# Three expert slots instead of six fetched beside the scatter of rows, and empty slots written during the second FFN

## The chip, the core and the metric

The kernel runs on one NeuronCore of a Trainium2 chip. The core has a matrix engine, TensorE (PE in the profile; its weight loads are listed apart as PEld), and VectorE (DVE), ScalarE (ACT), GpSimd (POOL) and SyncE (SP). Each engine takes its instructions in order from its own queue[...]. Transfers between memory and the on-chip buffers are done by 16 DMA engines[...]. SP does no arithmetic here and issues most of the transfers; ACT issues a few.

The metric is the device time of one execution in microseconds (us); for a kernel, the median of its runs.

## The reference

Four layers act on x, of 2 sequences, 1024 tokens each and 256 features (2048 tokens in all), in fp32. Every layer does

```
xn = layernorm(x)
x  = x + attention(xn) + ffn(xn)
```

with another attention and another FFN each time:

- layer 0: rotary attention with 16 heads of 16 features, and a gated FFN with 1024 hidden features (silu(gate) * up, then down)
- layer 1: rotary attention with 16 query heads and 4 key heads of 128 features, and again a gated FFN with 1024 hidden features
- layer 2: a state-space layer, and an FFN with weights rounded to -1, 0 and 1
- layer 3: an attention with states and actions of 32 features, and a mixture of 16 experts

The mixture of experts, cut to what matters:

```python
logits = x @ router_w
top_vals, top_ids = jax.lax.top_k(logits, 2)
probs = jax.nn.softmax(top_vals, axis=-1)
...
for e in range(16):
    h = silu(x @ W1[e]) @ W2[e]          # 256 -> 512 -> 256
    out = out + combine[:, e:e + 1] * h  # combine: probs at top_ids, else 0
```

Each token thus needs only two of the 16 experts.

## The kernel before, in words

x stays in the on-chip buffer in 16 tiles of 128 tokens (`xs`), worked on in four blocks of 512 tokens. A framework turns the Python loops into one queue for each engine, inserts the semaphores, and may reorder instructions by its own estimates, except between layers (`tc.no_sync_barrier()`) and where an order is asked for (`keep_in_program_order`, used for PE in layers 1 and 3).

**Norms.** `norm` (lines 95 to 122) takes for each block the statistics of four tiles on DVE (L102, L103), a square root on ACT (L105), a reciprocal on DVE (L107), the normalised tiles xn on DVE (L111), eight transposes on PE (L119) and two copies on ACT (L120) into `xnT`, the operand of the matmuls that follow.

**Gated FFN.** `ffn` (lines 160 to 181) runs over the four blocks; in each over eight "heads" of 128 hidden features: two matmuls into `g` (PSUM, tag "A", two buffers), two into `u` (tag "S", two buffers), the silu of g on ACT (L172) and the product with u on DVE (L174). Then the down projection and the addition to x (L132) follow. Layer 1's FFN is called by `swiglu(1, xnT, gu1, dn1)` at line 794, behind the whole attention of layer 1, whose last steps on ACT are the copies `oT` (L701). Ahead of that call SP is given the loads of layer 2's weights (lines 770 to 792).

**Experts.** Layer 3 spends matmuls only on the pairs of a token and one of its two experts, 4096 of them. The pairs are sorted into 47 slots of 128 rows; one slot belongs to one expert. `sent` is a tensor in memory with 47 * 128 rows of 258 numbers: 256 features, the row's number and its place. The parts:

- *Empty rows.* Not every row of a slot gets a pair. So `sent` is filled with empty rows long before: `none`, a tile of zeros, is written to all 47 slots (6016 KB), and `nowhere`, the two numbers of an empty row, behind it (47 KB). In the kernel before, this stands ahead of the norm of layer 1 (lines 558 to 565): three small POOL instructions and two transfers issued by ACT. The second transfer waits until the first has landed.
- *Scatter.* `send` (L1471) has POOL issue 32 indirect transfers, each of 128 rows to their places in `sent`. Around it, PE works on the attention of layer 3 for the second sequence (`attend(1, ...)`, softmax parts at L147 to L157, x at L1557).
- *Weights and rows.* `fetch(s)` has SP read the number of slot s's expert from the on-chip buffer (`value_load`) and load that expert's two weights, 512 KB each (`we<-in_L_W` at L56), into one of the seven buffers of the pool "ring". `rows_of(s)` has SP load the slot's 128 rows from `sent` (`xg<-sent`, 129 KB, five buffers); it waits for all 32 sends.
- *The loop.* Step s loads rows three slots ahead and weights six slots ahead, transposes the rows of slot s on PE (`tokens`), does the first matmul of slot s - 1 (`up`, hp, silu on ACT) and the second of slot s - 2 (`back`, eo, and an indirect transfer of the result rows into `done`). PE, held in program order (L1309, L1312), does this behind the attention of the second sequence's first four tiles. At the end the rest of the attention follows, and `collect` (L1721) adds the two results of every token to x.

Before the loop, all of SP's early transfers are asked for in this order:

```python
for s in range(6):
    fetch(s)
for s in range(3):
    rows_of(s)
```

Of the kernel before, what the change touches and what calls it, by code (L numbers as in the profile page):

```python
# [21 lines left out]
F32, I32, U32 = mybir.dt.float32, mybir.dt.int32, mybir.dt.uint32  # L22
# [5 lines left out]
P = 128  # L28
B, T, D = 2, 1024, 256
# [4 lines left out]
NSLOT = 47  # L34
# [5 lines left out]
C_ROW, C_NONE = 776, 778  # L40
# [5 lines left out]
def kernel(ctx: ExitStack, tc: tile.TileContext, a: dict, out: bass.AP):  # L46
    nc = tc.nc
    V, S, G, PE = nc.vector, nc.scalar, nc.gpsimd, nc.tensor
# [22 lines left out]
    cst = kept("cst", [P, C_COLS])  # L71
# [17 lines left out]
    sent = dram.tile([NSLOT * P, ROW], F32, tag="sent", name="sent")  # L89
# [48 lines left out]
    def work_pool(name):  # L138
        return tc.tile_pool(name=name, bufs=2, reuse_waits="tile")
# [57 lines left out]
    def swiglu(layer, xnT, gu, dn):  # L197
        with work_pool(f"ffn{layer}") as pool, psum_pool(f"ffn{layer}_ps") as psum:
            ffn(
                pool, psum, xnT, layer, [P] * 8,  # L200
                lambda k, h: gu[k][:, h * P : (h + 1) * P],
                lambda k, h: gu[k][:, 1024 + h * P : 1024 + (h + 1) * P],
                lambda h: dn[:, h, :],
                AF.Silu,
            )
# [12 lines left out]
    with work_pool("l0n") as pool, psum_pool("l0n_ps") as psum:  # L218
        _, xnT = norm(pool, psum, 0, 5)
    with work_pool("l0") as pool, tc.tile_pool(  # L220
        name="l0_ps", bufs=1, space=PSUM, reuse_waits="tile"
# [57 lines left out]
        def fetch(b, g):  # L279
            both = []  # L280
            for w_ in range(2):
                t_ = pool.tile([P, T], F32, tag="qk", name=f"qk{b}_{g}_{w_}", bufs=8)
                G.memset(t_, float(w_))
                for j in range(4):
                    load(t_[32 * j + 1 : 32 * j + 17, :], turned[b][w_].rearrange("(r h) t -> h r t", h=16)[4 * g + j])
                both.append(t_)
            qk[b, g] = both
# [267 lines left out]


    with work_pool("l1n") as pool, psum_pool("l1n_ps") as psum:
        none = pool.tile([P, D], F32, tag="none", name="none", bufs=1)
        G.memset(none, 0.0)
        nowhere = pool.tile([P, NSLOT, 2], F32, tag="nowhere", name="nowhere", bufs=1)  # L560
        G.memset(nowhere, -P)
        G.tensor_copy(nowhere[:, :, 0], cst[:, C_NONE : C_NONE + NSLOT])
        slots = sent.rearrange("(s p) d -> p s d", p=P)
        nc.scalar.dma_start(out=slots[:, :, :D], in_=none.unsqueeze(1).to_broadcast([P, NSLOT, D]))
        nc.scalar.dma_start(out=slots[:, :, D:], in_=nowhere)
        V.tensor_scalar_mul(w1k, w1k, 1.0 / math.sqrt(128.0))
        _, xnT = norm(pool, psum, 1, 5)
    with work_pool("l1") as pool, tc.tile_pool(
        name="l1_ps", bufs=1, space=PSUM, reuse_waits="tile"
# [3 lines left out]
        gu1, dn1 = load_swiglu(a["L1_gu"], a["L1_dn"], 1)  # L573
# [217 lines left out]
    load(nwD, a["L2_nwD"])  # L791
    nw, Dp = nwD[:, 0:16], nwD[:, 16:32]

    swiglu(1, xnT, gu1, dn1)
    tc.no_sync_barrier()


# [4 lines left out]
    with work_pool("l2n") as pool, psum_pool("l2n_ps") as psum:  # L802
        _, xnT = norm(pool, psum, 2, 5)
    with work_pool("l2") as pool, tc.tile_pool(
        name="l2_ps", bufs=2, space=PSUM, reuse_waits="tile"
# [509 lines left out]
    with work_pool("l3") as pool, tc.tile_pool(  # L1315
        name="l3_ps", bufs=2, space=PSUM, reuse_waits="tile"
# [315 lines left out]
        with work_pool("l3w") as wp:  # L1632
            with tc.tile_pool(name="at0_ps", bufs=2, space=PSUM, reuse_waits="tile") as psum:
                for _ in attend(0, psum, wp, range(QT)):
                    pass
                p1, p2 = shares()
                for _ in attend(1, psum, wp, range(4)):
                    pass

            with tc.tile_pool(name="moe_ps", bufs=2, space=PSUM, reuse_waits="tile") as psum:  # L1640
                w1s, w2s, xgTs, ehs = {}, {}, {}, {}

                def fetch(s):
                    ex = nc.sync.value_load(whoi[0:1, s : s + 1], min_val=0, max_val=15)
                    we = slot(f"we{s}")
                    w1s[s], w2s[s] = part(we, 0, 2, 512), part(we, 1024, 4, D)
                    load(w1s[s], a["L3_W1"][bass.ds(ex, 1)].rearrange("e (k p) m -> p (e k) m", p=P))
                    load(w2s[s], a["L3_W2"][bass.ds(ex, 1)].rearrange("e (k p) m -> p (e k) m", p=P))

                xgs, rows3 = {}, {}  # L1650

                def rows_of(s):
                    xgs[s] = wp.tile([P, ROW], F32, tag="xg", name=f"xg{s}", bufs=5)
                    load(xgs[s], sent[s * P : (s + 1) * P, :])

                def tokens(s):
                    xg = xgs.pop(s)
                    tp = psum.tile([P, 2, P], F32, tag="X", name=f"xgp{s}")
                    for k in range(2):
                        pe_t(tp[:, k, :], xg[:, k * P : (k + 1) * P])  # L1660
                    xgTs[s] = wp.tile([P, 2, P], F32, tag="xgT", name=f"xgT{s}", bufs=3)
                    V.tensor_copy(xgTs[s], tp)  # L1662

                    row = wp.tile([P, 1], F32, tag="row", name=f"row{s}", bufs=6)
                    G.tensor_scalar(
                        row, xg[:, D + 1 : D + 2], cst[:, C_ROW : C_ROW + 1], float(s * P),
                        op0=ALU.subtract, op1=ALU.is_equal,
                    )
                    G.tensor_scalar(
                        row, row, float(B * T), xg[:, D : D + 1], op0=ALU.mult, op1=ALU.add  # L1670
                    )
                    rows3[s] = wp.tile([P, 1], U32, tag="rowi", name=f"rowi{s}", bufs=10)
                    G.tensor_copy(rows3[s], row)

                def up(s):
                    hp = psum.tile([P, 4, P], F32, tag="H", name=f"hp{s}")
                    for h in range(4):
                        for k in range(2):
                            pe(hp[:, h, :], w1s[s][:, k, h * P : (h + 1) * P], xgTs[s][:, k, :], k == 0, k == 1)
                    ehs[s] = wp.tile([P, 4, P], F32, tag="eh", name=f"eh{s}", bufs=3)  # L1680
                    S.activation(ehs[s], hp, AF.Silu)

                def back(s):
                    op = psum.tile([P, D], F32, tag="E", name=f"eo{s}")
                    for h in range(4):
                        pe(op, ehs[s][:, h, :], w2s[s][:, h, :], h == 0, h == 3)
                    y = wp.tile([P, D], F32, tag="ey", name=f"ey{s}", bufs=8)
                    V.tensor_copy(y, op)
                    it = G.indirect_dma_start(
                        out=done, out_offset=bass.IndirectOffsetOnAxis(ap=rows3.pop(s)[:, 0:1], axis=0),  # L1690
                        in_=y, in_offset=None, bounds_check=2 * B * T + NSLOT * P - 1, oob_is_err=False,
                    )

                    tc.declare_no_dep(it.ins, group="results", reason="rows of different places")
                    tc.add_to_no_dep_group("results", it.ins)

                for s in range(6):
                    fetch(s)
                for s in range(3):
                    rows_of(s)  # L1700
                for s in range(NSLOT + 2):
                    if s + 3 < NSLOT:
                        rows_of(s + 3)
                    if s + 6 < NSLOT:
                        fetch(s + 6)
                    if s < NSLOT:
                        tokens(s)
                    if 0 <= s - 1 < NSLOT:
                        up(s - 1)
                    if s - 2 >= 0:  # L1710
                        back(s - 2)

            with tc.tile_pool(name="at1_ps", bufs=2, space=PSUM, reuse_waits="tile") as psum:

                ways = done[: 2 * B * T, :].rearrange("(r i p) d -> p i r d", r=2, p=P)

                def collect(i):
                    y = wp.tile([P, 2, D], F32, tag="back", name=f"back{i}", bufs=4)
                    load(y, ways[:, i])
                    for r, pr_ in enumerate((p2, p1)):  # L1720
                        V.scalar_tensor_tensor(  # L1721
                            xs[i], y[:, r], pr_[:, i : i + 1], xs[i], op0=ALU.mult, op1=ALU.add
                        )
                    nc.scalar.dma_start(out=osrc[i], in_=xs[i])

                for _ in attend(1, psum, wp, range(4, QT)):
                    pass
                for i in range(NT):
                    collect(i)
# [115 lines left out]
```

## Time and profile before

| | us |
|---|---|
| median of 3 runs | 3138.37 |
| the three runs | 3139.37, 3131.97, 3138.37 |
| the profiled execution | 3154.62 |
| its span (first to last instruction) | 3152.9 |

The profile is of one execution, and it is that execution's own time, not the median, to which its parts add up. Its TensorE clock was granted at 0.974 of full speed on the mean. It gives for each engine the busy time, the tenths of 40 equal slices in which it was busy, groups of equal instructions by source line, the waits by what ended them, and a timeline. "ACT L105 <- DMA sent<-none" is to be read as: the instruction of line 105 on ACT waited, and what came last was the transfer from `none` to `sent`. "remote" stands for a semaphore whose sender the profile does not name. In a timeline, a bracket at the end of a row holds the idle time of the engine ahead of that instruction and what ended it. Names end in q where an engine's queue of transfers is meant (SPq, ACTq).

Where the stretches of the change lie in the span:

| stretch | from, us | to, us |
|---|---|---|
| fill of `sent` to the first projection of layer 1 | 678 | 717 |
| FFN of layer 1 | 1670 | 1835 |
| scatter of rows | 2866 | 2913 |
| loop of experts on PE, first transposes | 2943 | |

### The profile page before, as it was taken

To read this page: it belongs to the slowest core of one execution; us is meant where nothing else is said; L and a number is where in the kernel's file an instruction comes from. 1 tells how busy PE (TensorE), PEld (TensorE's weight loads), DVE (VectorE), ACT (ScalarE), POOL (GpSimd) and SP (SyncE) were. 2 spreads that over 40 slices of the span, in tenths; PEclk is the share of its full clock that TensorE was granted. 3 is DMA by queue.
4 is the path that set the end of the run, shared out by engine and by line. 5 is a ranking of instruction groups with operands and counts; after the bars stand their busy time and mean duration, and the time that the engine had idled before them with its cause. 6 is when DMAs were issued, how large, how long until landed. Compare 5 with 4: busy or idle time off the path is not lost. (4 is left out here: it accounts for less than half of the span.)

```text
span 3152.9 us, 44146 instructions
## 1 busy us (share of the span) xinstructions
PE 2929.5 (93%) x16906; PEld 1996.2 (63%) x16906; DVE 1747.9 (55%) x3889; ACT 1198.4 (38%) x2129; POOL 911.2 (29%) x1224
## 2 busy tenths in 40 slices
PE   6999999969999999999999978999999999995998
PEld 5666666545655655655655555777777778554897
DVE  5665655326566566666551167677867774333223
ACT  2023333322333333333441155766666664212111
POOL 2021010103333333333320024444444443114342
PEclk9999999978999999999999988999999999998999
DMA  5000010050000000000000010000000000004696
GB/s 156 1 28 14 1 54 1 1 133 14 1 1 1 1 1 1 1 1 14 34 1 18 1 40 1 1 1 1 1 1 1 1 19 8 10 1 145 210 352 213
DMA packets 89442, 116.93 MB, mean 37 GB/s; under 512 B 13424, under 2 KB 70704, under 8 KB 87696
## 3 DMA queue, kind: packets, MB, share of 16 engines
q1 hardware_dynamic: 68768, 93.32, 9.1%
q10 hardware_dynamic: 16672, 10.40, 1.3%
q0 software_dynamic: 3792, 10.39, 0.9%
q8 instruction: 134, 2.20, 0.3%
q14 instruction: 76, 0.62, 0.1%
HBM read 91.20 MB, written 22.89 MB: 36 GB/s over the span
## 5 line engine op out<-in xcount | busy, mean ns | idle before, releaser
L157 ACT ACTIVATE pr<-sc,nmax 128x896 f32<-128x896 f32 (+7 forms) x272 | 201.2, 740 | 477.8 <-DVE nmax L156 376.8
L671 POOL TENSOR_SCALAR pr<-pr,r,gate 128x1024 f32<-128x1024 f32 (+7 forms) x256 | 209.8, 821 | 564.0 <-DVE r L670 536.1
L576 PE MATMUL sc<-kT,qT 128*128 128x512 f32 (+3 forms) x768 | 292.3, 492 | 21.5 <-ACT pr L157 21.5
L576 PE MATMUL op<-pT,v 128*128 128x512 f32 x576 | 292.9, 595 | 1.8 <-DVE pT L688 1.2
L342 ACT ACTIVATE pT<-sc 128x1024 f32<-128x1024 f32 (+1 forms) x160 | 150.1, 938 | 270.0 <-PE sc L248 270.0
L576 PEld LDWEIGHTS sc<-kT,qT 128*128 128x128 f32 x768 | 138.5, 192 | 157.0 <-issue 123.2
L156 DVE TENSOR_REDUCE nmax<-sc 128x1 f32<-128x896 f32 (+7 forms) x272 | 205.1, 757 | 7.9
L579 PEld LDWEIGHTS tp<-cst,pr 128*128 128x128 f32 x1152 | 140.2, 141 | 99.4 <-issue 70.6
L932 DVE SCALAR_TENSOR_TENSOR xp_ps<-xp,w2r,xp_ps 128x256 f32<-128x256 f32 x320 | 153.5, 486 | 56.7 <-ACT xp_ps L831 49.3
L248 PE MATMUL sc<-qk,qk 32*128 32x256 f32 (+1 forms) x1280 | 168.2, 380 | 9.4 <-ACT pT L342 8.8
L154 DVE TENSOR_TENSOR sc<-sc,cst 128x128 f32<-128x128 f32 x272 | 79.8, 296 | 174.1 <-PE sc L576 156.8
L957 POOL TENSOR_TENSOR dm<-cst,dA 128x512 f32<-128x512 f32 x128 | 133.3, 1050 | 112.1 <-PE lp L825 84.0
L579 PE MATMUL tp<-cst,pr 128*128 128x128 f32 x1152 | 164.3, 273 | 0.7 <-POOL pr L671 0.7
L345 POOL TENSOR_SCALAR_AFFINE_SELECT pT<-pT 128x512 f32<-128x512 f32 x64 | 40.6, 634 | 427.3 <-ACT pT L342 423.9
L248 PE MATMUL mx<-qk,qk 32*128 32x256 f32 (+1 forms) x1280 | 145.3, 389 | 10.8 <-DVE qk L329 2.9
L248 PEld LDWEIGHTS sc<-qk,qk 32*128 32x128 f32 x1280 | 104.4, 185 | 66.4 <-issue 31.2
L825 PE MATMUL lp<-dm,cst 128*128 128x512 f32 x256 | 132.5, 634 | 12.2 <-DVE ml L1022 7.0
L831 ACT ACT_TABLE_LOAD x105 | 134.7, 1283 | 4.8 <-PE zp L825 2.9
L831 ACT ACTIVATE xp<-xp_ps,w2r 128x256 f32<-128x256 f32 x160 | 90.2, 564 | 121.2 <-PE xp_ps L825 98.3
L825 PE MATMUL xp_ps<-xnT,w2x 128*128 128x256 f32 x512 | 128.5, 396 | 7.2 <-DVE xx L932 3.6
L688 ACT COPY pT<-tp 128x512 f32<-128x512 f32 x160 | 93.8, 586 | 105.0 <-PE tp L579 105.0
L576 PE MATMUL m<-w1o,oT 128*128 128x256 f32 x512 | 123.7, 385 | 4.1 <-DVE t2q L604 3.4
(321 smaller groups left out, 6025.3 us busy)
## 6 DMA issues: line engine op xcount, KB each, us to landing
we<-in_L_W SPq DMA_DIRECT2D x94, 512.0 KB
xg<-sent SPq DMA_DIRECT2D x47, 129.0 KB
sent<-none ACTq DMA_DIRECT2D x1, 6016.0 KB
gu<-in_L_gu SPq DMA_DIRECT2D x4, 1024.0 KB
back<-done SPq DMA_DIRECT2D x16, 256.0 KB
x<-in_x ACTq DMA_DIRECT2D x16, 128.0 KB
dn<-in_L_dn SPq DMA_DIRECT2D x2, 1024.0 KB
tabs<-in_L_rope SPq DMA_DIRECT2D x2, 1024.0 KB
```

The lines of the kernel that those rows point to most:

```text
L156: V.tensor_reduce(nmax, sc[:, :n], axis=AX.X, op=ALU.max, negate=True)
L157: S.activation(pr, sc[:, :n], AF.Exp, bias=nmax, accum_out=total)
L248: tc.keep_in_program_order(PE.matmul(out_, lhsT=lhsT, rhs=rhs, start=first, stop=last))
L342: S.activation(pT[:, :, :, :w], sc[:, :, :, :w], AF.Exp, scale=0.25)
L576: tc.keep_in_program_order(PE.matmul(out_, lhsT=lhsT, rhs=rhs, start=first, stop=last))
L579: tc.keep_in_program_order(PE.transpose(out_, in_, ident))
L671: G.tensor_scalar(pr[:, :n], pr[:, :n], r, gate[:, i, 4 * g + j : 4 * g + j + 1], op0=ALU.mult, op1=ALU.mult,)
L688: (V.tensor_copy if kb % 2 else S.copy)(made[kb], tp)
L825: tc.keep_in_program_order(PE.matmul(out_, lhsT=lhsT, rhs=rhs, start=first, stop=last))
L831: tc.keep_in_program_order(S.activation(*args, **kw))
L932: V.scalar_tensor_tensor(dst[:, n] if k == 2 else pp[:, n], xp[:, n, k : k + 256], cw[:, c : c + 1], pp[:, n], op0=ALU.mult, op1=ALU.add,)
L957: G.tensor_tensor(dm, le.unsqueeze(1).to_broadcast([P, 4, P]), dAc[:, 4 * g : 4 * g + 4].unsqueeze(2).to_broadcast([P, 4, P]), ALU.mult,)
```

## The change

Two things are changed. The filling of `sent` with empty rows is taken out of the norm of layer 1 and put around the FFN of layer 1, in a pool of its own; the instructions are the same. And of the first six slots' weights, three are asked for ahead of the first three slots' rows and three behind them.

```diff
     with work_pool("l1n") as pool, psum_pool("l1n_ps") as psum:
-        none = pool.tile([P, D], F32, tag="none", name="none", bufs=1)
-        G.memset(none, 0.0)
-        nowhere = pool.tile([P, NSLOT, 2], F32, tag="nowhere", name="nowhere", bufs=1)
-        G.memset(nowhere, -P)
-        G.tensor_copy(nowhere[:, :, 0], cst[:, C_NONE : C_NONE + NSLOT])
-        slots = sent.rearrange("(s p) d -> p s d", p=P)
-        nc.scalar.dma_start(out=slots[:, :, :D], in_=none.unsqueeze(1).to_broadcast([P, NSLOT, D]))
-        nc.scalar.dma_start(out=slots[:, :, D:], in_=nowhere)
         V.tensor_scalar_mul(w1k, w1k, 1.0 / math.sqrt(128.0))
         _, xnT = norm(pool, psum, 1, 5)
...
-    swiglu(1, xnT, gu1, dn1)
+    with work_pool("empty") as pool:
+        none = pool.tile([P, D], F32, tag="none", name="none", bufs=1)
+        G.memset(none, 0.0)
+        nowhere = pool.tile([P, NSLOT, 2], F32, tag="nowhere", name="nowhere", bufs=1)
+        G.memset(nowhere, -P)
+        G.tensor_copy(nowhere[:, :, 0], cst[:, C_NONE : C_NONE + NSLOT])
+        slots = sent.rearrange("(s p) d -> p s d", p=P)
+        nc.scalar.dma_start(out=slots[:, :, :D], in_=none.unsqueeze(1).to_broadcast([P, NSLOT, D]))
+        nc.scalar.dma_start(out=slots[:, :, D:], in_=nowhere)
+        swiglu(1, xnT, gu1, dn1)
     tc.no_sync_barrier()
...
-                for s in range(6):
+                for s in range(3):
                     fetch(s)
                 for s in range(3):
                     rows_of(s)
+                for s in range(3, 6):
+                    fetch(s)
                 for s in range(NSLOT + 2):
```

## The prediction

> **What bounds it now.** I read the page first. In the excerpt, "xN" counts instructions, and the row DMA gives the mean busy share of the 16 DMA engines in 40 slices of 78.8 us.
>
> ```profile
> span 3152.9 us, 44146 instructions
> ...
> PE 2929.5 (93%) x16906; PEld 1996.2 (63%) x16906; DVE 1747.9 (55%) x3889; ACT 1198.4 (38%) x2129; POOL 911.2 (29%) x1224
> ...
> DMA  5000010050000000000000010000000000004696
> ...
> sent<-none ACTq DMA_DIRECT2D x1, 6016.0 KB
> ```
>
> PE is the bound: 223 us of the span are not PE's. The change touches no arithmetic, so it can only fill or open gaps of PE. The DMA engines are busy at the start, at the norm of layer 1 (the ninth slice, where `sent<-none` lies) and from the 37th slice on, where rows are scattered and expert weights fetched. So I looked at PE's gaps in three stretches: norm 1, FFN 1, scatter.
>
> **Norm 1.** The view of waits from 660 to 720 us (total, times, longest), then ACT's timeline there (start, duration):
>
> ```profile
> ACT L105 <- DMA sent<-none: 28.0, 1, 28.0
> ...
> PE ln_ps L119 <- DVE xn L111: 19.9, 3, 16.7
> ```
> ```profile
> 678.02 0.39 ACTq L564 DMA_DIRECT2D sent<-none  x1
> 703.48 0.38 ACTq L565 DMA_DIRECT2D sent<-nowhere  x1
> 703.94 1.28 ACT L105 ACT_TABLE_LOAD   x1 [27.98 <-DMA sent<-none]
> 705.24 0.49 ACT L105 ACTIVATE sd<-mv,eps 128x4 f32<-128x4 f32 x2
> ```
>
> ACT issues the 6 MB fill, then must issue `nowhere`, which waits for the fill's completion; the square roots stand behind both. PE waits 16.7 us for xn, which needs them.
>
> *Gain of moving it.* DVE has x complete at 690.1. A block's four statistics take 1.74 us (0.87 a pair), so the first root could run at 692, with its table loaded before. Then DVE is the limit: 16 statistics and aggregates 7.0 us, 16 xn 5.5 (1.38 per four), four reciprocals 0.7, the w1k scale 0.7, together 13.9: 704 without gaps, 705.5 with the small waits before now between blocks. The last xn ends at 715.5 now. **Gain 10 us (9 to 11).** Behind it, the attention's tables are loaded when the norm frees their space and move with it; they now stand ahead of gu1 in SP's queue, not behind, which matters little: gu1 is used 950 us later. The memsets before the fill move on POOL to behind the last probability scaling (L671), where nothing waits for POOL.
>
> **FFN 1.** By the order of instructions in the changed kernel, the two fills stand on ACT directly behind the last copy of attention 1 (L701) and ahead of the silu table load and all 32 silus. ACT and PE in that stretch:
>
> ```profile
> 1666.79 0.58 ACT L701 COPY oT<-op 128x512 f32<-128x512 f32 x1 [2.64 <-PE op L576]
> 1667.39 1.28 ACT L172 ACT_TABLE_LOAD   x1
> 1671.96 0.60 ACT L172 ACTIVATE sg<-g 128x512 f32<-128x512 f32 x1 [3.29 <-PE g L129]
> ```
> ```profile
> 1669.94 1.98 PE L129 MATMUL g<-xnT,gu 128*128 128x512 f32 x4 [0.52 <-DVE x L132]
> 1671.76 1.88 PE L129 MATMUL u<-xnT,gu 128*128 128x512 f32 x4
> 1673.48 1.88 PE L129 MATMUL g<-xnT,gu 128*128 128x512 f32 x4
> ...
> 1676.91 1.88 PE L129 MATMUL g<-xnT,gu 128*128 128x512 f32 x4
> ```
>
> The last row is the third head; g and u have two PSUM buffers each, so it needs the first silu's read. *Cost, in the times of before:* the fill goes out at 1667.4. From its issue to the first activation behind `nowhere` was 27.2 us in norm 1 (705.24 - 678.02), table load included; the load beside it was 1 MB then, and w2z and the small tables, 1.35 MB, now. First silu 1694.6, done 1695.2; PE's third head starts at 1695.3 instead of 1676.9: **18.4 us**, 19.4 with the larger load beside. PE then restarts at half clock: after the two gaps of the scatter below, 4.4 and 5.2 us of its work ran so, half of it lost, 2.2 to 2.6 us. Nothing is won back: PE bounds FFN 1 (3.43 us per head, against 0.60 on ACT and 0.69 on DVE). **Cost 20.6 to 22, say 21.3; the net of the move is +11.3 us** (+9.6 to +13). A faster or slower fill moves both ends alike down to the point at which norm 1's gap closes, so the net hardly depends on it.
>
> Here a rule speaks for a shorter fill. The Trainium skill, "DMA: Bandwidth & Descriptors", section "Specifications", gives the transfers a ceiling of 435 GB/s. 6.16 MB would take 14.2 us; the row says 25.1 (678.4 to 703.5), 245 GB/s. With the ceiling, 10.9 us less, cost 10.4 and norm gain none, as DVE would free it: +10. I take the row.
>
> **Scatter.** POOL sends 32 times 128 rows from 2866.4 to 2907.9, 1.28 us each; SP issues weights beside it, 12 transfers of 512 KB, the first four at 2869.8 to 2872.5. Waits from 2866 to 2945, and stretches (time, then busy us of PE, PE's loads, DVE, ACT, POOL; clock, DMA share, GB/s):
>
> ```profile
> PE op L1309 <- DVE pT L149: 16.7, 2, 15.9
> ...
> PE op L1309 <- ACT pT L147: 14.7, 4, 13.5
> DVE x L1557 <- remote: 13.8, 2, 7.9
> ...
> DVE sc L154 <- remote: 9.8, 1, 9.8
> ```
> ```profile
> 2878.00:2893.00 15.00, 0.00 (x0) 0.00 (x0) 1.02 (x3) 0.89 (x2) 11.34 (x13) 0.59 0.87 288
> 2893.00:2900.00 7.00, 6.21 (x17) 4.32 (x17) 0.31 (x2) 0.00 (x0) 5.48 (x6) 0.66 0.74 248
> 2900.00:2913.00 13.00, 0.03 (x1) 0.03 (x1) 1.98 (x6) 1.58 (x3) 6.04 (x8) 0.67 0.53 168
> ```
>
> PE stands still for 15.9 + 13.5 = 29.3 us, and with the half clock loses 34. DVE and ACT wait there for semaphores that arrive 8 to 10 us after the matmul has ended ("remote"). *What three slots less can gain:* nothing if the scatter alone holds the semaphores up. If the weights do, not all 34: the first row tile now comes at 2942.95, and rows cannot be there before the last send lands and is fetched, about 2915. So **0 to 28 us in the profiled execution.** In timed runs less: plain register moves of SP take 0.69 us there instead of 0.03, which looks like the recording of the trace being held up, and the profiled run, 3154.6 us (1.7 outside its span), is 16.3 over the median. If that excess lies here, some 12 us remain at most.
>
> A rule speaks against any gain: "SBUF — State Buffer", section "SBUF: two separate sides", holds that engine ports and DMA ports are disjoint and neither slows the other. By it, this part is worth 0. The row shows late semaphores at a high DMA share, but the share alone is not the cause: the stall goes on at 0.53 (third row), with weights nearly done, and in the loop of experts the share is 0.89 over 176 us with PE busy for 175.9. Nearest to the stall, then, is the scatter, which stays. I take 0 to 2, **1 us**.
>
> *What it costs:* slots 3 to 5 now wait in SP's queue behind the rows, which wait for all sends: issued at 2912.6 instead of by 2910. At the loop's pace (1.31 MB per 3.73 us, 351 GB/s) 3.1 MB land by 2922; slot 3 is used three slots of 3.73 us after the first, 2926 at the earliest. Cover 4 us or more; nothing.
>
> **Sum.** -10 + 21.3 - 1 = +10.3. On the profiled run's own time 3165; on the median 3138.4, **3149 us**.
>
> **Rivals and chances.** About 0.3% (9.4 us: 3129 to 3147.8) separates a change from none.
> - *Forecast, 0.52*: stall hardly touched; 3146 to 3153.
> - *Part of the stall goes, 0.22*: the moves' +11.3 against 4 to 20 us; at 12, 3138. For it: the stall begins only when the weights have joined (share 1.0 at 2875). No change.
> - *The weights cause the stall and timed runs have it whole, 0.18*: PE reaches the rows at 2915, -28, 3122; up to 3129. It decides from a gain of 20.7 us. For it: nothing else starts at 2870. Against: the row at share 0.53 and the 16.3 us. Faster.
> - *Late weights, 0.08*: the ring lives from then on with three slots in hand instead of six; if each is 3 us late for three slots, +9 on top: 3158. Against: PE never waits for weights in the loop, with loads landing 13 us early.
>
> That the fill doesn't hold up FFN 1 is nearly excluded by ACT's order. Slower: 0.42 of the forecast and the last, 0.50; same: the rest of the forecast and the partial gain, 0.32; faster 0.18. The range, 3125 to 3155, leaves out half of the third case and the last.
>
> **What would show it.** In the changed profile: ACT's wait for the fill at L172, 24 to 27 us; a gap of 18 to 19 us of PE before the third g of FFN 1; PE's gap ahead of norm 1's transposes near 4 instead of 16.7 and the first projection near 707 instead of 717; at the scatter, two gaps of PE still near 29 together; none in the expert loop. The forecast is wrong if those two gaps are mostly gone and the timed runs follow, or if FFN 1's gap is under 10 us.

## The result, and the profile after

| | us |
|---|---|
| before, median of 7 runs (3129.02 to 3139.37) | 3134.86 |
| changed, median of 7 runs (3144.77 to 3152.62) | 3145.91 |
| ratio changed to before, 95% interval | 1.0038 (1.0025 to 1.0051) |
| profiled execution of the changed kernel; its span | 3144.93; 3143.2 |

The change made the kernel slower, by 11 us between the medians; the interval of the ratio is 8 to 16 us. 3149 had been forecast. The two profiled executions say the opposite: the changed kernel's span is 9.7 us *shorter*. That has to be explained too.

**The wait has moved from the norm to the FFN.** The view of waits of the changed kernel around FFN 1 (total, times, longest), then ACT's timeline there:

```profile
ACT L172 <- DMA sent<-none: 26.1, 1, 26.1
DVE hT L174 <- ACT sg L172: 25.6, 1, 25.6
PEld g L129 <- ACT sg L172: 19.2, 1, 19.2
PE g L129 <- ACT sg L172: 18.4, 1, 18.4
```
```profile
1660.86 0.39 ACTq L793 DMA_DIRECT2D sent<-none  x1
1687.06 0.38 ACTq L794 DMA_DIRECT2D sent<-nowhere  x1
1687.52 1.28 ACT L172 ACT_TABLE_LOAD   x1 [26.14 <-DMA sent<-none]
1688.81 1.08 ACT L172 ACTIVATE sg<-g 128x512 f32<-128x512 f32 x2
```

The issue of `nowhere` stands in ACT's queue ahead of the table load and the silus, so they stand still until the 6 MB have landed. The 26 us of ACT are the 25.5 of before, in another place. From the issue of the fill to the first silu it is 27.95 us. PE's timeline shows what they cost:

```profile
1669.20 1.88 PE L129 MATMUL u<-xnT,gu 128*128 128x512 f32 x4
1689.46 3.78 PE L129 MATMUL g<-xnT,gu 128*128 128x512 f32 x4 [18.39 <-ACT sg L172]
1693.04 2.28 PE L129 MATMUL u<-xnT,gu 128*128 128x512 f32 x4
1695.15 1.88 PE L129 MATMUL g<-xnT,gu 128*128 128x512 f32 x4
```

PE ran two heads ahead, stood for 18.39 us, and the next head's four matmuls then took 3.78 us instead of 1.88. This is the half clock: the granted TensorE clock is 0.50 from 1689.4 to 1693.0, and 1.00 ahead of the gap. In the norm of layer 1, on the other hand (PE's timeline; the last matmuls of layer 0, the first transposes, the first projection), the gap is 5.26 us instead of 16.7:

```profile
688.52 2.08 PE L248 MATMUL m<-w0b,oT 128*128 128x256 f32 x4 [0.52 <-DVE x L132]
695.85 4.10 PE L119 MATMUL ln_ps<-cst,xn 128*128 128x128 f32 x16 [5.26 <-DVE xn L111]
...
706.71 3.78 PE L568 MATMUL m<-xnT,w1kv 128*128 128x512 f32 x4 [0.25 <-ACT xnT L120]
```

**The scatter.** The same view of stretches as before (time, busy us of PE, PE's loads, DVE, ACT, POOL, then clock, DMA share, GB/s), over the time of the sends:

```profile
2880.00:2895.00 15.00, 13.78 (x63) 9.84 (x62) 10.24 (x29) 5.69 (x17) 11.38 (x12) 1.00 0.85 299
2895.00:2910.00 15.00, 14.36 (x73) 11.39 (x71) 5.00 (x11) 3.70 (x7) 11.34 (x13) 1.00 0.60 220
```

PE is busy where it stood before. Read alone, this says that fetching fewer slots cured a stall of 29 us, and the two spans agree. The timed runs do not. The experiments had to tell whether the six slots had ever caused that stall. And in the loop, where PE never waits for rows in the first profile of before, its timeline now shows such waits (`xgp` is the transpose of a slot's rows) with the clock halved behind them, 0.50 from 2945 to 2949:

```profile
2923.73 1.11 PE L1313 MATMUL xgp<-cst,xg 128*128 128x128 f32 x4 [3.31 <-DMA xg<-sent]
...
2945.18 0.66 PE L1313 MATMUL xgp<-cst,xg 128*128 128x128 f32 x2 [4.84 <-DMA xg<-sent]
2945.63 3.62 PE L1310 MATMUL hp<-xgT,we 128*128 128x128 f32 x16
2949.04 2.34 PE L1310 MATMUL eo<-we,eh 128*128 128x256 f32 x8
```

### The profile page after: what moved, and what is told of

Its sections match the earlier page's. It is cut to its first block, busy times and chain, and to the rows that moved or that the text cites. A ratio compares the mean times of both kernels' runs of the same rounds, so it can differ in the third digit from the quotient of the medians.

```text
span 3143.2 us, 44147 instructions
## 1 busy us (share of the span) xinstructions
PE 2935.6 (93%) x16906; PEld 1999.2 (64%) x16906; DVE 1747.5 (56%) x3889; ACT 1199.7 (38%) x2129; POOL 914.1 (29%) x1224
```

## The experiments

All ratios are to the kernel before, run on the same chip beside them: 7 runs for the changed kernel (above), and 70 with the median 3130.66 us or 48 with 3130.56 for the others. What each run's trace says of the four stretches, each worked out from starts in the timelines: "norm 1" from the end of the last addition of layer 0 to the first projection, "FFN 1" from its first g to the end of its last addition, "sends" from the first send to the first transpose of rows, "loop" from there to the end of the last hp. The first transpose waits for the first rows for 3.0 to 4.0 us in every trace but the first.

| kernel | ratio (95%) | norm 1 | FFN 1 | sends | loop |
|---|---|---|---|---|---|
| before, first profile | 1 | 27.0 | 165.9 | 76.5 | 173.0 |
| before, profiled again | - | 27.1 | 165.9 | 45.3 | 178.6 |
| changed | 1.0038 (1.0025 to 1.0051) | 15.7 | 186.7 | 45.4 | 182.5 |
| order of fetches only | 1.0018 (1.0006 to 1.0030) | 27.3 | 165.9 | 45.1 | 181.3 |
| fill moved only | 1.0034 (1.0021 to 1.0048) | 15.7 | 186.7 | 45.4 | 178.5 |
| changed, fills from SP | 0.9979 (0.9969 to 0.9989) | 15.7 | 165.9 | 45.1 | 181.5 |
| changed, small fill from SP | 0.9978 (0.9967 to 0.9988) | 15.7 | 165.9 | 45.2 | 181.4 |
| fills from SP, early reads, three slots | 0.9971 (0.9959 to 0.9984) | 15.3 | 165.9 | 45.4 | 180.5 |
| fills from SP, six slots | 0.9967 (0.9955 to 0.9979) | 15.7 | 165.9 | 45.3 | 178.1 |
| fills from SP, early reads, six slots | 0.9958 (0.9944 to 0.9971) | 15.7 | 165.9 | 46.1 | 175.3 |

**Each half alone.** The kernel before with the new order of fetches (the last part of the change's diff alone):

> Only the order of the first fetches is changed (three slots, rows, three slots); the fill stays in the norm of layer 1. Theory (the two gaps of 29 us at the scatter belong to the one profiled execution of before, which is 20 us over the median, and timed runs have none): 0 to -2 us against before, about 3134. Rival (six slots of weights hold up PE at the scatter in timed runs too, and the change gained there what the move lost beyond 11): -8 to -20 us, about 3115 to 3127.

Measured: 3135.18 us, ratio 1.0018, by the interval 2 to 9 us *slower*. Neither theory holds: the rival's gain is absent, and the order is not free. The fill moved, with six slots as before (the diff of the change without its last part):

> Only the fill is moved to the FFN of layer 1; six slots are fetched beside the scatter. Theory: +10 to +12 us against before, about 3146, the same as the whole change; PE's gap before the third head of FFN 1 18.4 us. If its profiled execution shows the gaps of the scatter, that execution lies as far above its other runs as the gaps are worth. Rival: +20 to +30 us, about 3155 to 3165, because the stall of the scatter is still there.

Measured: 3142.91 us, ratio 1.0034, by the interval 7 to 15 us slower: as the theory had it. Its trace has six slots beside the scatter and no stall there ("sends" 45.4 us). The halves alone add up to 0.52%, the whole is 0.38%; the intervals are wide enough for that.

**The stall at the scatter.** The kernel before, unchanged:

> The kernel before, unchanged, profiled once more. Theory (the gaps of 15.9 and 13.5 us at the scatter were an event of that one profiled execution): this execution comes out below 3145 us, without these gaps, with 45 us from the first send to the first transpose of rows instead of 76, and PE waits about 3 us for the first rows. Rival (six slots beside the scatter cause them): the gaps of 29 us are there again.

Measured: 3132.21 us, and in its stretches the scatter with the DMA share higher than in the stall of the first profile (0.87, then 0.53), and PE at work:

```profile
2882.00:2897.00 15.00, 14.65 (x71) 11.31 (x70) 6.68 (x15) 4.95 (x9) 11.50 (x12) 1.00 1.06 393
```

The DMA share is 1.06 with six slots in flight (above 1, so it is a rough measure), and PE is busy for 14.65 of 15 us. So neither the six slots nor busy DMA engines are enough to hold PE up. The gaps of the first profile belong to that one execution, 19.8 us above the median of before. They are in none of the nine other profiled executions of this study, four of which have six slots beside the scatter, and all of which have the 32 sends. What happened in it remains open: the late semaphores and the slow register moves of SP lie in the same 40 us, but nothing here could bring them back.

**What the wait in FFN 1 is.** Both fills issued by SP, at the same place of the program:

```diff
-        nc.scalar.dma_start(out=slots[:, :, :D], in_=none.unsqueeze(1).to_broadcast([P, NSLOT, D]))
-        nc.scalar.dma_start(out=slots[:, :, D:], in_=nowhere)
+        nc.sync.dma_start(out=slots[:, :, :D], in_=none.unsqueeze(1).to_broadcast([P, NSLOT, D]))
+        nc.sync.dma_start(out=slots[:, :, D:], in_=nowhere)
```

> The changed kernel with its two fills issued by SP instead of ACT, at the same place in the program. Theory (the cost is the wait on ACT, not the transfer): the 18.4 us gap and its half clock are gone, -20 to -21 us against the changed kernel, about 3125, -10 against before. Rival (6 MB written beside FFN 1 hold up its loads or PE itself): gain of less than 10 us, about 3136 or more.

Measured: 3123.87 us, ratio 0.9979; FFN 1 is back at 165.85 us to the hundredth, with 6 MB written beside it. Against the changed kernel's 1.0038 that is 0.59%, 18 us; the stretch alone gives 20.8. And with only the second line of the diff changed, the 6 MB still from ACT:

> The changed kernel with only the second, small fill (47 KB) issued by SP; the 6 MB fill stays on ACT. Theory (ACT stands still because the second issue waits for the first transfer's landing): PE's gap before the third head is gone, as with both fills from SP, -18 to -21 us against the changed kernel. Rival (issuing the 6 MB transfer itself occupies ACT): the gap stays, 0 to -2 us.

Measured: 3125.21 us, ratio 0.9978, the same. ACT's timeline of this kernel:

```profile
1659.03 0.39 ACTq L793 DMA_DIRECT2D sent<-none  x1
1659.57 1.28 ACT L172 ACT_TABLE_LOAD   x1
1664.13 0.60 ACT L172 ACTIVATE sg<-g 128x512 f32<-128x512 f32 x1 [3.28 <-PE g L129]
```

The table load follows the 6 MB issue at once. What stopped ACT, in both kernels, was the 47 KB transfer that has to wait for the other one's landing. SP issues it in this run at 1686.28, and nothing waits for SP then.

**What the order of fetches costs.** The loop takes 181.3 to 182.5 us in the four kernels with the new order, and 178.1 to 178.6 in the three with the old one (the early reads, and the first profile of before, set aside): the order costs 3 to 4 us. PE's timeline at the rows of the sixth slot, first of the kernel with only the order changed, then of the one with only the fill moved, last of before profiled again:

```profile
2924.04 1.89 PE L1309 MATMUL eo<-we,eh 128*128 128x256 f32 x8
2931.11 0.66 PE L1312 MATMUL xgp<-cst,xg 128*128 128x128 f32 x2 [5.18 <-DMA xg<-sent]
2931.56 3.28 PE L1309 MATMUL hp<-xgT,we 128*128 128x128 f32 x16
```
```profile
2942.01 1.89 PE L1310 MATMUL eo<-we,eh 128*128 128x256 f32 x8
2945.29 0.41 PE L1313 MATMUL xgp<-cst,xg 128*128 128x128 f32 x2 [1.39 <-DMA xg<-sent]
2945.54 1.95 PE L1310 MATMUL hp<-xgT,we 128*128 128x128 f32 x16
```
```profile
2934.54 0.41 PE L1312 MATMUL xgp<-cst,xg 128*128 128x128 f32 x2 [2.89 <-DMA xg<-sent]
2934.79 1.95 PE L1309 MATMUL hp<-xgT,we 128*128 128x128 f32 x16
```

With the new order PE waits 5.18 us and then runs at half clock; with the old one it waits 1.39 or 2.89 us, and 1.2 us once more at a later slot, and keeps the full clock. The cause stands on SP. Its queue, in the changed kernel, over 14 us at that place, in the view of the line with `value_load` (duration in ns, lowest, median and highest):

```profile
L1645 SPq TENSOR_LOAD <-whoi x25: 262/263/275, 2928.9 to 2942.4; - x25
L1645 SPq FUSED_REGOPS  x25: 147/147/152, 2929.2 to 2942.7; - x25
L1645 SPq SEQ_ASSERT  x25: 18/18/18, 2929.4 to 2942.9; - x25
```

The framework has gathered 25 of the reads of expert numbers in one place, between the rows of the fifth and of the sixth slot, 0.56 us each, 14 us in all. Whatever SP has to issue ahead of them moves the sixth slot's rows. In the traces of order alone and of fill alone:

```
SP's issues, us from the first transpose of rows (W: half a slot's weights, R: rows)
six slots:    ... W-28.9 | R-2.2 R-1.8 R-1.3 R-0.9 W0.4 W1.0 R1.4              [25 reads] R16.2
three slots:  ... W-33.5 | R-2.0 R-1.6 R-1.2 W-0.5 W0.6 W1.2 R1.6 W3.0 W3.5 R4.0 [25 reads] R18.7
```

Three transfers have been moved behind the sends (the framework kept nine ahead of them, four and a half slots, not three), and the sixth slot's rows go out 2.5 us later. With six slots the wait is there too, but shorter, as the timelines above show. To test whether the reads are at the root, SP reads the numbers ahead, while it waits for the sends, first with three slots:

```diff
                 for s in range(3):
+                    expert(s)
                     fetch(s)
+                for s in range(3, NSLOT):
+                    expert(s)
                 for s in range(3):
                     rows_of(s)
```

(`expert(s)` is the `value_load` of `fetch(s)`; the fills are from SP.)

> As the fill from SP, and SP reads the expert numbers of slots 3 to 46 directly behind the first three slots' weights, where it waits for the sends, instead of 25 of them in a row between the fifth and the sixth slot's rows. Theory (these 25 reads, 14 us, are what PE's second wait for rows, 4.8 us, and the half clock after it come from): -6 to -8 us against the fill from SP, about 3118. Rival (rows are late because of the transfers queued ahead of them, not because of SP): 0 to -1 us; or the 44 reads, 25 us, end after the sends have landed, and the rows come later: +1 to +5 us.

Measured: 3122.3 us, ratio 0.9971 against 0.9979 without it: 2.5 us, within the intervals, and less than expected. The wait at the sixth slot is gone, but another one is there, at the fourth, again with half clock behind it:

```profile
2914.08 0.66 PE L1313 MATMUL xgp<-cst,xg 128*128 128x128 f32 x2 [3.63 <-DMA xg<-sent]
2914.53 3.62 PE L1310 MATMUL hp<-xgT,we 128*128 128x128 f32 x16
```

SP now really keeps to three slots, so six transfers of 512 KB are issued between the third and the fourth slot's rows: those rows go out 4 us later than the third slot's, behind 3 MB on the way, and take 8.6 us from issue to landing, where the third slot's took 2. So the rival was right for this kernel: with the reads out of the way, the transfers ahead of the rows make them late. Six slots, then, first with the reads where they were, and then with 41 of them ahead of the rows:

> The fills from SP at FFN 1, and the order of fetches of before (six slots beside the scatter). Theory (the new order of fetches costs 3 us: SP issues three more transfers between the sends' landing and its 25 reads, so the rows of the sixth slot come later, and PE's pause is long enough to halve its clock): -3 to -4 us against the fill from SP with three slots, about -10 against before; PE's waits for rows in the loop 1.2 to 1.4 us each instead of 5.2. Rival (the order of fetches is worth nothing): the same as with three slots, -6.6 against before.

Measured: 3120.48 us, ratio 0.9967. The point values lie 0.12%, 4 us, apart from the three-slot kernel, as expected, but the intervals overlap; it is the loop, 178.1 against 181.5 us, that carries it.

> As the one before it, and SP reads the expert numbers of slots 6 to 46 (41 reads, 23 us) while it waits for the sends. Theory: no wait of PE for rows in the loop after the first; the loop from the first transpose to the last first matmul 175 to 176 us instead of 178.5 with six slots and 181 with three; about -13 against before, the fastest. Rival (reads end after the sends have landed): the first rows come later by 1 to 5 us, about -8 against before.

Measured: 3120.45 us, ratio 0.9958. PE's waits in this kernel, from the first rows to the end of the loop, are one line, the first rows:

```profile
PE xgp L1313 <- DMA xg<-sent: 4.0, 1, 4.0
```

The loop takes 175.3 us, as expected, 3 us less than with the reads in it; the first rows come 0.7 us later. With the reads early in both, six slots are 5 us faster in the loop than three (175.3 against 180.5). So the reads and the transfers ahead of the rows each make rows late, and the order of fetches costs time with either. Against the same kernel without early reads the timed runs cannot tell it apart (medians 3120.45 and 3120.48). One of its 15 runs took 6607.89 us, which the ratio leaves out and nothing here explains. Both kernels with six slots and the fills from SP are faster than before by 7 to 18 us (their two intervals), and than the changed kernel by some 22 to 25.

## Why the prediction was right, and where it was not

- *Norm 1, gain 10 (9 to 11)*: 11.4 us (27.1 to 15.7), a little over the range. DVE ran what I had added up to 13.9 us without the gaps I had allowed for; the last xn ended 13.6 us after the last addition of layer 0.
- *FFN 1, cost 20.6 to 22*: 20.8 us (186.7 against 165.9): a gap of 18.39, where 18.4 stood, and 2.4 for the half clock. The fill took 26.2 us beside 1.35 MB, 235 GB/s. So the row of the trace was the right measure, and not the ceiling of 435 GB/s from the Trainium skill, "DMA: Bandwidth & Descriptors", section "Specifications".
- *Net of the move +11.3*: +9.4 by the stretches, +10.6 by the ratio of the kernel with this half alone. The reasons given carry it: in the norm DVE's own work takes the place of part of the wait, in FFN 1 PE is the bound and wins nothing back.
- *Scatter, gain 0 to 2*: none; right in size, and the case made against the weights holds (the excess of the profiled run lay there, and busy DMA engines do not hold PE up). The Trainium skill's rule in "SBUF — State Buffer", section "SBUF: two separate sides", agrees with the row of before profiled again: 1.06 of share and PE busy at 14.65 of 15 us. But the scatter, which I had called nearest to the stall, is not its cause either: the sends stand in all ten profiles, the stall in one. So the sign "two gaps of PE still near 29 together" did not come. I had also left some 12 us of the stall to timed runs as a possibility; there was nothing of it.
- *Later weights, cost nothing*: this step failed. "Slots 3 to 5 now wait in SP's queue behind the rows" was wrong in its count, since three transfers of 512 KB were moved, not six; and "cover 4 us or more; nothing" looked at the landing of weights alone. The weights were in time, and PE never waited for them. What was late were the rows behind them in SP's queue, which also held 14 us of reads. Against the sign "none in the expert loop", PE has a wait of 4.84 us there. The trace of before has the same reads, from 2915.3 to 2929.5, hidden there because PE came late from the stall. The step cost 3 to 4 us where I had put nothing.

So the +10.3 of the sum was made of +11.3 and -1, and the measured 11 to 12 of about +9.4 and +3: the direction and the main term were right, and two errors of 2 and 4 us cancelled in part, which was luck. These stretches are also not all that differs between the two traces: attention 1, between norm 1 and FFN 1, took 957.2 us in the changed kernel and 952.9 in before profiled again, at a granted clock of 0.987 and 0.991. It is the same work in all ten, and took 953.7 to 957.8 us in the seven kernels with the fill moved, 952.9 to 953.5 in the three others. Whether the move has a part in that is open, since two of those seven, with the same code up to layer 3, stand 3.6 us apart (957.8 and 954.2). The last rival, late weights, was the nearest to what happened, with the wrong transfer in it.

## What to carry to other kernels

A transfer that must wait for another's landing should be issued by a queue on which nothing waits; here 47 KB in ACT's queue cost 11 us in the norm, 21 in the FFN, and nothing in SP's. When a stretch of a profile holds more lost time than the timed runs can hold, profile the same kernel again before explaining it. And count on an issuing engine everything that it does, register reads too: they set when the next transfer goes out.

## What was not expected of the hardware

- One execution in which, for some 40 us, semaphores of PE arrived 8 to 10 us late and register moves of SP took 0.69 instead of 0.03 us, without a cause that could be repeated.
- Reading one number from the on-chip buffer into a register costs SP 0.56 us (0.26 for the load, the rest for the steps around it).
- The executions of one kernel differ by some 10 us either way. Norm 1 and FFN 1 repeat to 0.4 us in all kernels alike in them, but the stretch of layer 2 from its first dp to its last xp_ps, the same work in all ten profiles, took 727.3 to 734.4 us. The granted TensorE clock goes with it: 0.975 on the mean in the shortest and 0.965 in the longest, and the length times the share not granted is 18.2 and 25.5 us, as far apart as the lengths. The 70 runs of before show the same: the median of the six with a mean clock of 0.973 is 3141.0 us, that of the 14 with 0.977 is 3129.8. So effects of 3 us are to be read in the stretches that the change touches, not in the medians.
